# An attention kernel at TensorE's bound: order of cut score products, places of the x load and outputs, start and tail

## The chip, the cores and the metric

The kernel runs on one core of one Trainium2 chip. The metric is the device time of one execution in microseconds (us); lower is better. A median of several executions is quoted for each kernel with its extremes. Ratios are of the mean time of one kernel's fast runs over that of the other's in the same rounds, so they are not quite the ratios of the medians. For kernels that were only looked at (one time, one profile), the state of the run is unknown and no interval exists.

All runs of all kernels in this document gave correct results.

## The reference, cut to what matters

```python
# x: (32, 256, 32, 32): 32 images, 256 channels, S = 1024 positions; 8 heads of 32
xn = group_norm(x, G=32)                       # 8 channels a group
q, k, v = q_w @ xn + q_b, kv_w @ xn + kv_b     # (256, 1024) each
scores = q_h.T @ k_h / sqrt(32)                # per head, positions strictly before only
attn = softmax(scores);  attn[masked] = 0
out = x + attn @ v                             # residual
```

## The kernel before

The 32 images are worked off one behind the other, with 12 visits for each, 384 in all. A visit is one block of scores, one projection of the next image, and the products with v of the visit before. Four heads share TensorE, each in its own 32 rows ("row group"). The parts that the change and the argument touch:

```python
# A score piece is 512 columns; in 4 of 12 visits it is cut into 384 + 128 (two key blocks).
def piece(g, hf, k, part=None):
    d = k - hf * BPH
    if d == 1:
        blocks = [(k, slice(P, HALF), slice(P, HALF)), (k + 2, slice(0, P), slice(3 * P, HALF))]
    ...

def scores(b, full, half, between=()):
    ...
    first = [scores_of((b, half), short[:, j % 2, 1, :], j) for j in (2, 3)]   # 2 short products
    for j in range(4):
        scores_of((b, full), pairs[j // 2][:, j % 2, :], j)    # all blocks of head j inside
    ...                                                        # 2 more short products, then 3 exponentials on ScalarE

# The sums of the exponentials: VectorE adds up pieces (values), two DMAs that add fold them
# to 32 partitions (fold), another stacks four of them (stack), TensorE sums them (pd).
def sum_folded(b):
    pd = misc(f"pd_{b}")
    sum_keys(pd, live.pop(("folded", b)), ..., of_rows=pick_half)
    ...
# Their inverses: 4 DMAs of 256 KB bring them back, spread over partitions
def invert(b, ns):
    ...
    for n in ns:
        nc.sync.dma_start(out=inverses(b, n), in_=by_half[n].unsqueeze(1).broadcast_to([4, HD, HALF]))
# and the outputs use them on VectorE:
def finish(b, n, within=slice(0, HALF)):
    ...
    nc.vector.tensor_mul(rb, num[:, within], rb)                                    # L463
    nc.vector.scalar_tensor_tensor(rb, rb, v_bias_col[...], xt[...], ALU.add, ALU.add)  # L464
    nc.sync.dma_start(out=x_out[b, :, g, cols], in_=rb)

# Which visit does what, relative to the image's first visit (N = 12)
PREPARE = (-18, -17, -9, -9, -8, -8, -7, -6)     # statistics (2), mean, dev, var, rstd, normalised x (2)
FINISH = ((N + 12, N + 12, N + 13, N + 14), ...) # the four outputs
when(max(first - 2 * N + 3, 0), lambda b=b: load(b))
```

`misc` is a single PSUM buffer, which the small products share with some projections. x loads, outputs, stacked sums and inverses all go through the one queue of SyncE, in the order in which they were issued. SyncE waits there for what a transfer needs, and what stands behind waits with it.

## Time and profile before

| | before |
|---|---|
| median of 6 runs | 1877.49 us (1874.42 to 1880.56) |
| profiled execution | span 1874.0 us |
| start until the first score block | 19.02 us |
| an image (12 visits) | 57.20 us |
| cut / whole score block, until the next product | 1.600 / 1.503 us |
| images over 57.2 us | 3 of 29, together 2.3 us over |
| last score block until the end | 23.72 us |

The times in the lower rows are my readings of when each score block starts in the trace; the images are the second to the thirtieth (the first and the thirty-first are longer in both kernels, by 3.5 to 3.9 us). One row of the view of waits matters little at first sight, and much later. Its columns behind the colon are us in total, how many times, and the longest:

```profile
DVE rb L463 <- DMA rb<-inverses: 11.3, 11, 2.5
```

VectorE (DVE) waits 11 times for the fetched inverses before it can compute an output.

### The profile page before, as it was taken

To read this page: it belongs to the slowest core of one execution; us is meant where nothing else is said; L and a number is where in the kernel's file an instruction comes from. 1 tells how busy PE (TensorE), PEld (TensorE's weight loads), DVE (VectorE), ACT (ScalarE), POOL (GpSimd) and SP (SyncE) were. 2 spreads that over 40 slices of the span, in tenths; PEclk is the share of its full clock that TensorE was granted. 3 is DMA by queue.
4 is the path that set the end of the run, shared out by engine and by line. 5 is a ranking of instruction groups with operands and counts; after the bars stand their busy time and mean duration, and the time that the engine had idled before them with its cause. 6 is when DMAs were issued, how large, how long until landed. Compare 5 with 4: busy or idle time off the path is not lost.

```text
span 1874.0 us, 54145 instructions
## 1 busy us (share of the span) xinstructions
PE 1850.8 (99%) x23410; PEld 950.6 (51%) x23410; DVE 1573.4 (84%) x1604; ACT 1413.7 (75%) x1775; POOL 765.5 (41%) x741
## 2 busy tenths in 40 slices
PE   8999999999999999999999999999999999999997
PEld 4555555555554555555555545455555555455543
DVE  3778988888988889888889888898888888888878
ACT  5777777777777777777777777777777777777775
POOL 1443443434434434434344344343343443443413
PEclk9999999999999999999999999999999999999998
DMA  3446665666666666665666656766556666666412
GB/s 119 69 79 144 138 145 118 117 137 138 140 123 127 125 140 139 145 121 111 137 138 142 145 105 123 140 138 148 117 114 140 138 143 116 133 123 140 95 50 81
DMA packets 77516, 233.41 MB, mean 125 GB/s; under 512 B 19808, under 2 KB 20832, under 8 KB 61912
## 3 DMA queue, kind: packets, MB, share of 16 engines
q0 software_dynamic: 15360, 94.39, 34.4%
q1 hardware_dynamic: 60280, 134.72, 24.7%
q8 instruction: 185, 3.03, 0.7%
q10 hardware_dynamic: 1632, 0.79, 0.1%
q14 instruction: 59, 0.48, 0.1%
HBM read 68.41 MB, written 35.62 MB: 56 GB/s over the span
## 4 chain that ended last, share of the span: by engine, by line
PE 97%; DVE 1%; DMA 0%; ACT 0%; issue 0%; ACTq 0%; DVEq 0%
PE sT L277 31%; PE acc L353 26%; PE pp L169 25%; PE ppv L169 13%; PE pd L390 2%; DVE e L358 1%; DMA wn<-in_L_conv_kv_w_dram 0%; DVE rb L464 0%; DVE rb L463 0%; DVE rb L478 0%; ACT e L331 0%; PE pv L169 0%; PE busy L155 0%; ACT k L231 0%; PE pm L169 0%
## 5 line engine op out<-in xcount | busy, mean ns | idle before, releaser
L331 ACT ACTIVATE e<-sT 128x1024 f32<-128x1024 f32 x768 | 748.3, 1022 | 365.4 <-PE sT L277 283.2
L358 DVE TENSOR_TENSOR e<-e,eh 128x1024 f32<-128x1024 f32 x382 | 534.5, 1413 | 247.2 <-PE acc L353 215.1
L292 POOL TENSOR_SCALAR_AFFINE_SELECT e<-e 128x512 f32<-128x512 f32 (+1 forms) x256 | 359.4, 1404 | 678.5 <-ACT e L331 657.9
L358 DVE TENSOR_TENSOR e<-e,e 128x1536 f32<-128x1536 f32 x381 | 618.0, 1622 | 16.9 <-POOL e L292 2.6
L277 PE MATMUL sT<-q,k 32*128 32x256 f32 (+3 forms) x7168 | 617.6, 460 | 0.8 <-ACT k L231 0.8
L277 PEld LDWEIGHTS sT<-q,k 32*128 32x128 f32 x7168 | 463.4, 184 | 163.7 <-ACT q L231 50.6
L169 PE MATMUL pp<-xn,wT 128*32 128x512 f32 x4096 | 492.2, 598 | 0.0
L353 PE MATMUL acc<-e,v 128*32 128x512 f32 (+2 forms) x4096 | 401.1, 486 | 0.0
L329 ACT ACTIVATE eh<-sT 128x1024 f32<-128x1024 f32 x384 | 395.6, 1030 | 0.0
L371 POOL DMA_DIRECT2D e<-e x240 | 199.5, 892 | 388.0 <-PE sT L277 159.5
L169 PE MATMUL ppv<-wT,xn 128*32 128x256 f32 x4096 | 247.3, 382 | 0.0
L353 PEld LDWEIGHTS acc<-e,v 128*32 128x32 f32 x4096 | 132.9, 110 | 223.6 <-issue 201.1
L353 PE MATMUL acc<-eh,v 128*32 128x256 f32 x3072 | 224.4, 379 | 0.0
L169 PEld LDWEIGHTS pp<-xn,wT 128*32 128x32 f32 x4096 | 107.0, 109 | 218.2 <-issue 199.3
L353 PEld LDWEIGHTS acc<-eh,v 128*32 128x32 f32 x3072 | 98.5, 110 | 164.2 <-issue 152.6
L169 PEld LDWEIGHTS ppv<-wT,xn 128*32 128x32 f32 x4096 | 120.2, 109 | 102.0 <-issue 32.1
L292 POOL TENSOR_SCALAR_AFFINE_SELECT eh<-eh 128x512 f32<-128x512 f32 x128 | 160.6, 1255 | 0.1
L464 DVE SCALAR_TENSOR_TENSOR rb<-rb,v_bias_col,x 128x512 f32<-128x512 f32 (+1 forms) x127 | 114.1, 898 | 4.5
L463 DVE TENSOR_TENSOR rb<-num,rb 128x512 f32<-128x512 f32 (+1 forms) x127 | 90.4, 711 | 11.6 <-DMA rb<-inverses 11.3
L231 ACT ACTIVATE k<-pp,qk_bias 128x512 f32<-128x512 f32 x128 | 89.4, 698 | 13.5 <-PE pp L169 12.4
L214 DVE TENSOR_SCALAR xn<-x,mean,rstd 128x512 f32<-128x512 f32 x128 | 96.7, 796 | 2.0 <-POOL rstd L207 2.0
L231 ACT ACTIVATE q<-pp,qk_bias 128x512 f32<-128x512 f32 x128 | 89.9, 702 | 4.0 <-PE pp L169 4.0
(69 smaller groups left out, 515.2 us busy)
## 6 DMA issues: line engine op xcount, KB each, us to landing
e<-e POOLq DMA_DIRECT2D x120, 512.0 KB, 8.0
x<-in_x_dram SPq DMA_DIRECT2D x64, 512.0 KB
out_dram<-rb SPq DMA_DIRECT2D x127, 256.0 KB
rb<-inverses SPq DMA_DIRECT2D x126, 256.0 KB
e<-e POOLq DMA_DIRECT2D x120, 256.0 KB, 5.0
folded<-e SPq DMA_DIRECT2D x120, 256.0 KB
rows<-sums SPq DMA_DIRECT2D x31, 32.0 KB
inverses<-inv SPq DMA_DIRECT2D x31, 32.0 KB
```

Of the source, the lines that this page charges most:

```text
L169: nc.tensor.matmul(out[part], lhsT=lhsT[:, part], rhs=rhs, start=start, stop=stop, skip_group_check=True)
L214: nc.vector.tensor_scalar(live["xn", b][:, g, cols], live["x", b][:, g, cols], mean[:, g : g + 1], rstd[:, g : g + 1], ALU.subtract, ALU.mult,
L231: nc.scalar.activation(live[key][:, cols], pp, AF.Identity, bias=qk_bias[:, n, g : g + 1], scale=(SCALE, 1.0)[n],)
L277: ins = nc.tensor.matmul(pair[:, cols], lhsT=live["k", b, g][rows, kb * P : (kb + 1) * P], rhs=live["q", b, g][rows, hf * HALF + of.start ...
L292: nc.gpsimd.affine_select(out=diagonal, in_=diagonal, pattern=[[0, 4], [0, n], [1, P]], compare_op=ALU.is_gt, fill=0.0, base=0, channel_mu ...
L329: exp = nc.scalar.activation(eh.rearrange("p (n bank) q -> p bank n q", n=2), short, AF.Exp)
L331: nc.scalar.activation(e[:, 2 * a : 2 * a + 2, :], pairs[a], AF.Exp)
L353: nc.tensor.matmul(acc[HD * j : HD * (j + 1), of], lhsT=live["v", b][:, kb, h * HD : (h + 1) * HD], rhs=e[:, j, cols], start=first, stop=l ...
L358: nc.vector.tensor_add(total[:, :, of], total[:, :, of], e[:, :, cols])
L371: nc.gpsimd.dma_start(out=total[:rows], in_=total[rows : 2 * rows], accum_op=ALU.add)
L463: nc.vector.tensor_mul(rb, num[:, within], rb)
L464: nc.vector.scalar_tensor_tensor(rb, rb, v_bias_col[:, g : g + 1], xt[:, g, cols], ALU.add, ALU.add)
```

## The change

Four parts. (1) In cut visits the long pieces of all four heads come first, then the short ones. (2) At the start x of the first image is fetched alone, the weights stand behind it on the same queue, the three weight transposes follow one another, and smaller filler products are to keep TensorE's clock up. (3) At the end one more addition of exponentials is done by TensorE instead of VectorE, the sum that waits for VectorE stands last, and half of the last output goes to GpSimd and ScalarE. (4) In every image the x load goes out three visits later, statistics, the second half of normalised x and the outputs one or two visits later.

```diff
@@ (1) scores
-            for j in range(4):
-                scores_of((b, full), pairs[j // 2][:, j % 2, :], j)
+            for n in range(len(full[4])):
+                for j in range(4):
+                    scores_of((b, full), pairs[j // 2][:, j % 2, :], j, n)
@@ (2) start
-        for b in range(min(2, B)):
-            load(b)
+        load(0)
-                nc.scalar.dma_start(out=live["wn", n], in_=w.rearrange("(o p) c -> p o c", p=P))
+                nc.sync.dma_start(out=live["wn", n], in_=w.rearrange("(o p) c -> p o c", p=P))
-                nc.tensor.matmul(pt[:, 0, :C], lhsT=ident, rhs=live["wn", 0][:, 0, :], start=True, stop=True)
+                nc.tensor.matmul(pt[:, 0, :P], lhsT=ident, rhs=ident, start=True, stop=True)
...
             load_weights()
-            turn_weights(0)
+            if B > 1:
+                load(1)
+            junk = small.tile([P, 1], F32, tag="most", name="junk")
+            nc.scalar.activation(junk, ones, AF.Exp)
+            keep_busy(11)
             for g in range(NG):
                 norm_channels(0, g)
-            keep_busy(2)
+            nc.vector.tensor_scalar_mul(qk_bias[:, 0, :], qk_bias[:, 0, :], SCALE)
             norm_mean(0)
-            turn_weights(1)
+            keep_busy(3)
             ...
-            turn_weights(2)
-            keep_busy(4)
+            for n in range(3):
+                turn_weights(n)
+            keep_busy(3)
@@ (3) tail
-            finish(b, 3, both[0])
+            finish_aside(b, 3, both[0])
...
-                    for pc in products[(i - 1) % N]:
-                        values((i - 1) // N, pc, i < B * N - 1)
+                for n, pc in enumerate(products[(i - 1) % N] if i else ()):
+                    summed = i < B * N - 2 or (i == B * N - 2 and n == 0)
+                    values((i - 1) // N, pc, summed)
+                    if i == B * N:
+                        sum_piece(B - 1, pc, stop=n == 1)
+                        if n == 0:
+                            sum_total(B - 1)
+                if i == B * N - 1:
+                    for n, pc in enumerate(products[N - 2] + products[N - 3][1:]):
+                        sum_piece(B - 1, pc, start=n == 0)
@@ (4) places
-        PREPARE = (-18, -17, -9, -9, -8, -8, -7, -6)
+        PREPARE = (-16, -15, -9, -9, -8, -8, -7, -5)
-        FINISH = ((N + 12, N + 12, N + 13, N + 14), (N + 7, N + 7, N + 8, N + 9))
+        FINISH = ((N + 13, N + 13, N + 14, N + 15), (N + 7, N + 7, N + 8, N + 9))
-                    when(max(first - 2 * N + 3, 0), lambda b=b: load(b))
+                    when(max(first - 2 * N + 6, 0), lambda b=b: load(b))
```

More of the change, by code (lines that the diff above doesn't have):

```diff
@@ L151, in keep_busy @@
         def keep_busy(n):
-            pt = ps_s.tile([P, 2, HALF], F32, tag="sT", name=f"busy_{n}")
+            pt = ps_s.tile([P, 2, HALF], F32, tag="sT", name="busy")
             for _ in range(n):
-                nc.tensor.matmul(pt[:, 0, :C], lhsT=ident, rhs=live["wn", 0][:, 0, :], start=True, stop=True)
+                nc.tensor.matmul(pt[:, 0, :P], lhsT=ident, rhs=ident, start=True, stop=True)
         def spare(name):
@@ L270, in piece, with scores_of @@
             return g, hf, k, part, tuple(blocks)
-        def scores_of(pc, pair, j):
+        def scores_of(pc, pair, j, n=0):
             b, (g, hf, k, part, blocks) = pc
             rows = slice(HD * j, HD * (j + 1))
-            for kb, cols, of in blocks:
-                ins = nc.tensor.matmul(
-                    pair[:, cols], lhsT=live["k", b, g][rows, kb * P : (kb + 1) * P],
-                    rhs=live["q", b, g][rows, hf * HALF + of.start : hf * HALF + of.stop],
-                    start=True, stop=True, skip_group_check=True,
-                )
-            return ins
+            kb, cols, of = blocks[n]
+            return nc.tensor.matmul(
+                pair[:, cols], lhsT=live["k", b, g][rows, kb * P : (kb + 1) * P],
+                rhs=live["q", b, g][rows, hf * HALF + of.start : hf * HALF + of.stop],
+                start=True, stop=True, skip_group_check=True,
+            )
         def mask(pc, e):
@@ L393, in sum_keys, with sum_piece, sum_total @@
                 )
-        def sum_pieces(b, pieces, start, stop):
+        def sum_piece(b, pc, start=False, stop=False):
             if start:
                 live["pd", b] = misc(f"pd_{b}")
-                sum_keys(live["pd", b], live["sum", b, NG - 1, NH - 1], slice(0, HALF), slice(0, HALF), True, False)
-            for pc in pieces:
-                e = live.pop(("e", b, pc))
-                for kb, cols, of in pc[4]:
-                    sum_keys(live["pd", b], e, cols, of, False, stop and pc is pieces[-1])
+            e = live.pop(("e", b, pc))
+            for kb, cols, of in pc[4]:
+                sum_keys(live["pd", b], e, cols, of, start, stop)
+        def sum_total(b):
+            sum_keys(
+                live["pd", b], live["sum", b, NG - 1, NH - 1], slice(0, HALF), slice(0, HALF), False, False
+            )
         def sums(b, g, hf):
             n = NH * g + hf
-            total = live.pop(("sum", b, g, hf))
+            den = small.tile([P, HALF], F32, tag="den", name=f"den_{b}_{n}")
             if (b, n) == (B - 1, 3):
@@ L412, in sums @@
                 pd = misc(f"pd_{b}_{n}")
-                sum_keys(pd, total, slice(0, HALF), slice(0, HALF))
-            den = small.tile([P, HALF], F32, tag="den", name=f"den_{b}_{n}")
+                sum_keys(pd, live.pop(("sum", b, g, hf)), slice(0, HALF), slice(0, HALF))
             if b == B - 1 and n >= 2:
@@ L467, in finish, with finish_aside @@
             nc.sync.dma_start(out=x_out[b, :, g, cols], in_=rb)
+        def finish_aside(b, n, within=slice(0, HALF)):
+            g, hf = divmod(n, NH)
+            cols = slice(hf * HALF + within.start, hf * HALF + within.stop)
+            num, rb, xt = live["num", b, n], live["rb", b, n][:, within], live["x", b]
+            nc.gpsimd.tensor_tensor(rb, num[:, within], rb, ALU.mult)
+            nc.gpsimd.tensor_tensor(rb, rb, xt[:, g, cols], ALU.add)
+            nc.scalar.activation(rb, rb, AF.Identity, bias=v_bias_col[:, g : g + 1])
+            if cols.start == 0:
+                nc.scalar.copy(rb[:, 0:1], xt[:, g, 0:1])
+            nc.sync.dma_start(out=x_out[b, :, g, cols], in_=rb)
         def check_here(n, ok):
@@ L478, in invert_here @@
             nc.vector.reciprocal(rb[:, within], live["den", n][:, within])
-        def finish_aside(b, n):
-            g, hf = divmod(n, NH)
-            cols = slice(hf * HALF, (hf + 1) * HALF)
-            num, rb, xt = live["num", b, n], live["rb", b, n], live["x", b]
-            nc.gpsimd.tensor_tensor(rb, num, rb, ALU.mult)
-            nc.gpsimd.tensor_tensor(rb, rb, xt[:, g, cols], ALU.add)
-            nc.scalar.activation(rb, rb, AF.Identity, bias=v_bias_col[:, g : g + 1])
-            if hf == 0:
-                nc.scalar.copy(rb[:, 0:1], xt[:, g, 0:1])
-            nc.sync.dma_start(out=x_out[b, :, g, cols], in_=rb)
         def end_last(b):
@@ L561, in unshifted @@
             norm_rstd(0)
-            turn_weights(2)
-            keep_busy(4)
+            for n in range(3):
+                turn_weights(n)
+            keep_busy(3)
             for hf in range(NH):
                 norm_apply(0, slice(hf * HALF, (hf + 1) * HALF))
-            nc.vector.tensor_scalar_mul(qk_bias[:, 0, :], qk_bias[:, 0, :], SCALE)
             units = projections(0)
@@ L584, in unshifted @@
                     v = first + (N if last and n == 3 else SUMS[n])
-                    if last and n == 3:
-                        for i in (N - 1, N):
-                            when(first + i, lambda b=b, i=i: sum_pieces(b, products[i - 1], i == N - 1, i == N), after)
                     if late:
@@ L618, in unshifted @@
                     f()
-                if i:
-                    for pc in products[(i - 1) % N]:
-                        values((i - 1) // N, pc, i < B * N - 1)
+                for n, pc in enumerate(products[(i - 1) % N] if i else ()):
[8 more added lines that the diff above has]
+                        sum_piece(B - 1, pc, start=n == 0)
                 for f in after.pop(i, ()):
```

## The prediction

> **What bounds the kernel now.** I read the page's busy times and chain of waits first. They say whether one engine is the bound over the whole span.
>
> ```profile
> PE 1850.8 (99%) x23410; PEld 950.6 (51%) x23410; DVE 1573.4 (84%) x1604; ACT 1413.7 (75%) x1775; POOL 765.5 (41%) x741
> ...
> PE 97%; DVE 1%; DMA 0%; ACT 0%; issue 0%; ACTq 0%; DVEq 0%
> ```
>
> TensorE is busy for 99% of the span and makes 97% of the chain that ended last. So outside the first 19 us and the last 25 us only TensorE's own time counts, and work moved between the other engines is worth nothing as long as it stays late enough. I checked this from the starts of the 384 visits (a visit is one block of scores, then one projection, then the value products of the visit before): 12 visits make one of the 32 images, and an image takes 57.20 us almost every time. Only three of the images from the second on differ: 57.93, 58.63 and 57.32, in sum 2.3 us. So there is one fixed cost per visit. Next I read the timeline of TensorE over a few visits, to see how much of a visit is which product.
>
> ```profile
> 943.08 1.67 PE L277 MATMUL sT<-q,k 32*128 32x256 f32 x24
> 944.68 1.92 PE L169 MATMUL pp<-xn,wT 128*32 128x512 f32 x16
> ...
> 947.83 1.57 PE L277 MATMUL sT<-q,k 32*128 32x256 f32 x16
> 949.33 1.92 PE L169 MATMUL pp<-xn,wT 128*32 128x512 f32 x16
> ```
>
> Columns are start, length, engine, line, product, count. Both score blocks stream the same columns. The x24 one has its long piece cut into 384 and 128 columns, and holds TensorE 944.68 - 943.08 = 1.60 us until the projection begins; the x16 one has it whole, and holds 949.33 - 947.83 = 1.50 us. Over all visits I find 1.600 against 1.503 us, nearly without spread. There are 4 cut visits per image, 128 in all.
>
> Last, I read the chain in order of time at both ends, where TensorE does wait:
>
> ```profile
> 1.82 8.96 DMA wn<-in_L_conv_kv_w_dram
> ...
> 10.83 1.12 PE wt L148 x4
> 11.95 2.69 PE busy L155 x8
> 14.64 3.62 PE pp L169 x32
> ```
>
> The start waits for the third weight matrix, because weights and two images of x are fetched at once; then 8 filler products stand ahead of the first projection.
>
> ```profile
> 1854.07 1.95 DVE e L358
> ...
> 1856.07 3.67 PE pd L390 x24
> 1859.74 1.68 PE acc L353 x24
> 1861.41 1.34 PE pd L390 x24
> ...
> 1867.04 1.68 DVE rb L478
> ```
>
> At the end TensorE waits for VectorE's last addition (L358) before it sums the exponentials (pd), and the final divisions are then serial on VectorE. The table of stretches adds why the 3.67 us are so long:
>
> ```profile
> 1857.00:1860.40 3.40, 3.40 (x28) 1.24 (x24) 3.40 (x2) 0.00 (x0) 3.30 (x3) 0.50 0.12 46
> ```
>
> The third column from the right is the granted clock: it was halved after the 2.05 us wait at 1854 to 1856.
>
> **What the Trainium skill says.** "TensorE: Matmul & The Clock Gate", Part 3, The mechanism, states that a weight load overlaps running products only where the row group differs, and that matmuls start and end strictly in program order. The trace agrees on the first as far as row groups overlap (in the x16 block matmuls of different row groups start 7 ns apart), and contradicts the second: in the x24 block of 943.08 the second 384-column matmul starts 13 ns after the first, while the 128-column one that stands between them in the program starts 0.76 us later. So each row group (one head) works off its own sequence. The same page, Part 1, says that the clock falls to half after an idle window; the stretch above shows 0.50. "DMA: Bandwidth & Descriptors", Issuing engines are not separate DMA queues, says transfers from all queues interleave on the same 16 engines; this trace agrees: x on one queue and weights on another land alternately, x's second half at 6.6, the last weights at 10.8 us. "SBUF — State Buffer", Who interferes with whom, says a VectorE operation with two inputs in SBUF and a GpSimd operation exclude each other; the multiplication L463 takes 0.68 us, but 1.17 us at 1861.12 beside GpSimd's L486.
>
> **The change part by part.**
> (1) Score order. The new order of instructions shows the four heads' 384-column matmuls first, then the four 128-column ones; before, each head's 384 and 128 stood together. Single records of the visit at 943.08 say what that costs. The first short products (heads 2 and 3) hold their row groups until 943.62. The weights for head 2's 384 columns are loaded at 943.41, but those for head 3's only at 943.62, just after head 2's first piece began, although head 3's row group could have taken them at 943.41. Head 3's matmul there is 584 ns long against 481 ns for those with weights in place: 0.103 us of bare weight load. I read this as head 2's second piece standing in front and blocking the issue of head 3's first. In the x16 block, where nothing stands between, both heads load together (952.370 and 952.377). In the new order nothing stands between either, so a cut visit should cost what a whole one does: 1.600 - 1.503 = 0.097 us. Times 128, less the two last ones that wait for ScalarE anyway: 126 x 0.097 = 12.2 us, all on the path. An image becomes 57.20 - 4 x 0.097 = 56.81 us.
> (2) Start. x is fetched alone first, and the weights follow on the same queue. With x undisturbed its second half should land about 1.2 us earlier (estimate: 1 MB at the 340 to 400 GB/s that the packets show, from 2.2 us), so the statistics and normalised x come some 1 us earlier. The weights, 0.75 MB right behind x and ahead of the next image, should be there by 8 to 8.5 us instead of 10.8. The filler ahead of the projection shrinks from 8 records of 256 columns (2.69 us) to 6 of 128, about 0.8 us; but all 12 transposes (1.12 us for each of three groups) now follow one another. From the statistics' second sum at about 9 us: 3 x 1.1 + 0.8 = 4.1, so the first projection at 12 to 13 instead of 14.6. I take 2.2 us.
> (3) Tail. One addition of 1024 elements more (the 1.95 us one) goes to TensorE as four products of 256 columns, 0.43 us; the sum that waits for VectorE moves behind the other products. TensorE no longer idles for 2.05 us and keeps its clock: from 1853.95, 1.7 of pd + 0.97 acc + 0.97 pd + 0.86 total + 0.43 + 0.43 gives 1859.3 against 1862.7. But VectorE still has the 3.34 us reciprocal and two operations beside GpSimd's; it gains 1 to 2 us, and sets the end. One half of the last output goes to GpSimd and ScalarE: 0.42 + 0.48 us off VectorE's serial end, hidden behind its second reciprocal (1.75 us). Together 2.5 us.
> (4) x three visits later, statistics, normalised x and outputs spread. Off the path: the x load moves from 16.8 us after an image's start to about 29, its statistics are due over two visits (some 12 us) later, and its packets ended 5 to 9 us after the issue in most images, 13 us in the worst, which VectorE's slack (84% busy) should absorb. What it can give is the 2.3 us of the three long images: there the x load went out at 19.3 to 20.3 instead of 16.8 us, the transfers of folded sums followed behind it, and the sum over them (pd) started up to 1.41 us late. After the change x stands behind those transfers in the queue. The profiled execution without those is about 1876.05 - 2.3 = 1873.8, close to the fastest of the three timed runs (1874.42), so the median of 1879.02 probably has more of them.
> Sum: 12.2 + 2.2 + 2.5 = 16.9 us, from 1874 to 1879 depending on how many late sums remain: 1857 to 1862.
>
> **Rivals.** (a) The 1.60 us come from the 8 additional weight loads and matmuls as such, not from their order. Then (1) gives nothing and the time is about 1869. For it: there are 8 records more. Against it: three of the four row groups end on time, and only one shows the bare load. (b) ScalarE takes over: a visit's first matmul needs the score buffer that the last exponential of the visit before releases. In the visit at 952.05 that exponential ended at 956.15, 4.10 us in, and the visit lasts 4.22: 0.12 us of room, but that visit isn't shortened. The cut ones fall from 4.744 to 4.65 and have 0.5 us of room. If it bound after all, half of (1) would be lost: 1865. (c) The moved x load now meets other folds (at 29.6 us in an image) and holds up GpSimd's queue, which waited up to 8.8 us for such transfers, and with it the masks. TensorE shows no such wait now, and masks have some 4 us of room; if it happened in every image at 0.3 us, 10 us would go and the time be 1868. (d) All late sums vanish and the start gains 3 us: 1853.
>
> **Range and chances.** I centre on 1858: the fixed gain is well founded, and the late sums probably mostly go. Rivals (a) to (c) are the upper end and beyond, (d) the lower. Faster by 2% would need under 1841.4, 16 us below my centre, more than both ends can give; slower by 2% (over 1916.6) would need a new wait of 58.6 / 384 = 0.15 us in every visit.
>
> **What would show it.** The x24 score blocks should last 1.50 us to the next product, the image 56.8 us, with no weight load standing bare before a 384-column matmul; the first projection at 12 to 13 us; no wait of TensorE for L358 at the end and a granted clock of 1.00 there; no image over 57.2. I am wrong if cut visits stay at 1.60, if TensorE shows new waits for ScalarE or masks, or if images vary more than before.

## The result

The changed kernel takes 1860.22 us in the median of 6 runs (1858.67 to 1861.51), against 1877.49 us in the same rounds; the ratio of fast runs is 0.9909 with an interval of 0.9896 to 0.9922. The profiled execution has a span of 1856.6 us. So the result lies within 2%, 2.2 us from the predicted 1858. The runs also lie closer together: 2.8 us between extremes instead of 6.1.

| profiled execution | before | after | difference |
|---|---|---|---|
| start until the first score block | 19.02 | 16.74 | 2.28 |
| first to last score block | 1831.27 | 1819.06 | 12.21 |
| last score block until the end | 23.72 | 20.80 | 2.92 |
| span | 1874.0 | 1856.6 | 17.4 |
| an image | 57.20 | 56.85 | 0.35 |
| cut score block | 1.600 | 1.512 | 0.088 |
| images over the shortest by over 0.05 us | 3 (2.3 us) | 0 | 2.3 |

The row from first to last score block is made up of 29 images at 0.349 each (10.1 us), the three long images (2.3 us) and the first image (0.3 us), less 0.55 us by which the last image got longer (48.73 to 49.28 us up to its last score block; I did not follow that up).

The page's busy times and its chain by engine, after:

```profile
PE 1838.8 (99%) x23440; PEld 932.9 (50%) x23440; DVE 1556.5 (84%) x1601; ACT 1414.5 (76%) x1777; POOL 774.5 (42%) x743
...
DVE 2%; PE 2%; issue 0%; ACT 0%; DVEq 0%
```

TensorE is still the bound, with 12.0 us less to do and 30 records more. The second line misleads if compared with before's: here the program that follows the chain back stopped at 1766.0 us, so only the last 91 us are in these shares of the span. Busy time and the starts of the visits have to carry the reading.

TensorE's timeline over two visits, one cut and one whole (start, length, engine, line, product, count):

```profile
906.62 1.58 PE L276 MATMUL sT<-q,k 32*128 32x256 f32 x24
908.13 1.92 PE L168 MATMUL pp<-xn,wT 128*32 128x512 f32 x16
911.27 1.57 PE L276 MATMUL sT<-q,k 32*128 32x256 f32 x16
912.77 1.93 PE L168 MATMUL pp<-xn,wT 128*32 128x512 f32 x16
```

The x24 block now holds TensorE 908.13 - 906.62 = 1.51 us until the projection begins, the x16 block 1.50, though the first still has eight records more (four products; the trace has two records of each).

The start, from the timeline:

```profile
5.16 1.29 DVE L178 BATCH_NORM_STATS2 st<-x 128x6 f32<-128x512 f32 x2 [5.16 <-DMA x<-in_x_dram]
7.06 1.29 DVE L178 BATCH_NORM_STATS2 st<-x 128x6 f32<-128x512 f32 x2 [0.37 <-DMA x<-in_x_dram]
10.10 1.53 PE L147 MATMUL wt<-ident,wn 128*128 128x128 f32 x12
11.37 1.92 DVE L213 TENSOR_SCALAR xn<-x,mean,rstd 128x512 f32<-128x512 f32 x4 [1.59 <-POOL rstd L206]
11.46 0.90 PE L154 MATMUL busy<-ident 128*128 128x128 f32 x6
12.29 3.64 PE L168 MATMUL pp<-xn,wT 128*32 128x512 f32 x32
```

The brackets give the wait before an instruction and what ended it. The statistics start at 5.16 and 7.06 us; in before they started at 4.47 and 6.62. So x came later, not earlier. Normalised x is begun at 11.37 (before: 11.41). What is gained stands on TensorE: all 12 transposes in 1.53 us, then 0.83 us of filler (12.29 - 11.46) instead of 2.69, and the first projection at 12.29 instead of 14.57.

The tail, from the chain in order of time (start, length, engine, tile, line):

```profile
1840.29 3.27 DVE rb L493
1843.58 1.68 DVE rb L466
1845.28 1.65 DVE rb L467
...
1848.06 1.67 DVE rb L493
1849.73 1.69 DVE rb L493
```

The chain now runs through VectorE's reciprocals (L493) and one output, as the prediction said: VectorE sets the end, not TensorE. In the table of stretches the third column from the right is the granted clock:

```profile
1842.00:1846.00 4.00, 3.16 (x56) 1.35 (x44) 3.93 (x3) 1.21 (x4) 3.92 (x4) 1.00 0.08 26
```

It is 1.00 where before had 0.50. And VectorE's wait for the inverses has gone. In the page's groups the last column is the idle time in front of a group: 0.1 us over 126 multiplications, where the view of waits gave 11.3 us for the kernel before:

```profile
L466 DVE TENSOR_TENSOR rb<-num,rb 128x512 f32<-128x512 f32 x126 | 87.8, 696 | 0.1
```

### The profile page after: what moved, and what is told of

Same layout as the page of the kernel before. It is cut to its first block, busy times and chain, and to the rows that moved or that the text cites. A ratio compares the mean times of both kernels' runs of the same rounds, so it can differ in the third digit from the quotient of the medians.

```text
span 1856.6 us, 54181 instructions
## 1 busy us (share of the span) xinstructions
PE 1838.8 (99%) x23440; PEld 932.9 (50%) x23440; DVE 1556.5 (84%) x1601; ACT 1414.5 (76%) x1777; POOL 774.5 (42%) x743
## 3 DMA queue, kind: packets, MB, share of 16 engines
q1 hardware_dynamic: 61096, 135.51, 24.7%
## 5 line engine op out<-in xcount | busy, mean ns | idle before, releaser
L359 DVE TENSOR_TENSOR e<-e,eh 128x1024 f32<-128x1024 f32 x381 | 524.0, 1389 | 260.4 <-PE acc L354 186.2
L359 DVE TENSOR_TENSOR e<-e,e 128x1536 f32<-128x1536 f32 x381 | 629.4, 1652 | 15.4 <-POOL e L290 1.0
L290 POOL TENSOR_SCALAR_AFFINE_SELECT e<-e 128x512 f32<-128x512 f32 (+1 forms) x256 | 368.3, 1439 | 617.7 <-ACT e L332 595.1
L276 PE MATMUL sT<-q,k 32*128 32x256 f32 (+3 forms) x7168 | 606.3, 458 | 0.8 <-ACT k L230 0.8
L276 PEld LDWEIGHTS sT<-q,k 32*128 32x128 f32 x7168 | 444.1, 184 | 169.9 <-ACT eh L330 65.6
L290 POOL TENSOR_SCALAR_AFFINE_SELECT eh<-eh 128x512 f32<-128x512 f32 x128 | 165.1, 1289 | 0.1
L467 DVE SCALAR_TENSOR_TENSOR rb<-rb,v_bias_col,x 128x512 f32<-128x512 f32 x126 | 95.9, 761 | 4.5
L466 DVE TENSOR_TENSOR rb<-num,rb 128x512 f32<-128x512 f32 x126 | 87.8, 696 | 0.1
L178 DVE BATCH_NORM_STATS2 st<-x 128x6 f32<-128x512 f32 x128 | 81.8, 681 | 5.5 <-DMA x<-in_x_dram 5.5
```

The source lines that it names most:

```text
L178: nc.vector.bn_stats(st[:, c, :], live["x", b][:, g, c * HALF : (c + 1) * HALF])
L276: return nc.tensor.matmul(pair[:, cols], lhsT=live["k", b, g][rows, kb * P : (kb + 1) * P], rhs=live["q", b, g][rows, hf * HALF + of.start ...
L290: nc.gpsimd.affine_select(out=diagonal, in_=diagonal, pattern=[[0, 4], [0, n], [1, P]], compare_op=ALU.is_gt, fill=0.0, base=0, channel_mu ...
L359: nc.vector.tensor_add(total[:, :, of], total[:, :, of], e[:, :, cols])
L467: nc.vector.scalar_tensor_tensor(rb, rb, v_bias_col[:, g : g + 1], xt[:, g, cols], ALU.add, ALU.add)
```

## The experiments

Names beginning with `a_` are the changed kernel with an edit, those with `b_` the kernel before with one. Each kernel's median is compared with the runs of before in the same call: 1878.03 us (14 runs, for `a_by_head`, `b_long_first`, `a_split23`, `a_split01`), 1878.24 us (one run, for `a_all_cut_long`, `a_all_cut_head`, `b_no_filler`, `a_old_fetch`) and 1877.04 us (27 runs, for the other four). Runs called timed were in the fast state. The readings of the traces in one table:

| kernel | median us | first score block | cut block | an image | long images (us over) | last score block to end |
|---|---|---|---|---|---|---|
| before | 1877.49 | 19.02 | 1.600 | 57.20 | 3 (2.3) | 23.72 |
| after | 1860.22 | 16.74 | 1.512 | 56.85 | 0 | 20.80 |
| a_by_head | 1871.18 | 18.12 | 1.600 | 57.20 | 0 | 21.58 |
| b_long_first | 1876.48 | 19.56 | 1.512 | 56.85 | 8 (13.8) | 23.31 |
| a_split23 | 1861.25 | 18.12 | 1.519 | 56.87 | 0 | 21.56 |
| a_split01 | 1871.12 | 18.04 | 1.600 | 57.20 | 0 | 21.58 |
| a_all_cut_long | 1868.69 | 18.04 | 1.512 | 57.15 | 0 | 19.93 |
| a_all_cut_head | 1893.97 | 18.23 | 1.600 | 57.92 | 0 | 21.36 |
| b_no_filler | 1876.09 | 17.68 | 1.600 | 57.20 | 4 (3.7) | 23.62 |
| a_old_fetch | 1864.24 | 20.99 | 1.512 | 56.85 | 0 | 22.16 |
| a_old_spread | 1873.01 | 18.00 | 1.512 | 56.85 | 8 (14.7) | 20.82 |
| a_old_outputs | 1863.17 | 18.99 | 1.512 | 56.85 | 8 (6.6) | 20.81 |
| a_old_tail | 1863.68 | 18.98 | 1.512 | 56.85 | 0 | 23.48 |
| a_outputs_aside | 1866.44 | 19.03 | 1.512 | 56.85 | 0 | 27.73 |

A median covers several executions (one where the kernel was only looked at), the other columns one profiled execution each.

### a_by_head: the order alone undone

```diff
-            for n in range(len(full[4])):
-                for j in range(4):
+            for j in range(4):
+                for n in range(len(full[4])):
                     scores_of((b, full), pairs[j // 2][:, j % 2, :], j, n)
```

> The changed kernel with only the order of the cut score pieces put back (each head's 384 and 128 columns together). Theory (a head's second piece standing in front keeps the next head's weights from loading): the 128 cut score blocks go from 1.512 back to 1.600 us, an image from 56.85 to 57.20, the time from 1860.2 to about 1871.3. Rival (the steady gain came from the moved loads and outputs, and the order only went along): cut blocks may change but the time stays within 3 us of 1860.

Measured, timed: 1871.18 us (1870.86 to 1872.36, 5 runs), ratio to before 0.9959 (0.9944 to 0.9975). That is 11.0 us more than the changed kernel. Every cut block is back at 1.600 us and every image at 57.20, with the same products, columns and loads. So the order, not the number of products, costs these 0.088 us per cut visit.

### b_long_first: the order alone done

```diff
-            for j in range(4):
-                scores_of((b, full), pairs[j // 2][:, j % 2, :], j)
+            for n in range(len(full[4])):
+                for j in range(4):
+                    scores_of((b, full), pairs[j // 2][:, j % 2, :], j, n)
```

> The kernel before with only the score order of the change. Theory: cut blocks 1.512 us, an image 56.85 us, time 1877.5 - 11 = 1866.5, but single longer images (late sums, up to 1.4 us each) remain because x and the outputs are where they were; start and end as before (first score block at 19.0 us, about 23.7 us from the last score block to the end). Rival: no gain without the other parts, 1877.

Measured, timed: 1876.48 us (1873.56 to 1884.21, 10 runs), ratio 0.9992 (0.9976 to 1.0008). This was the surprise of the study. The cut block is 1.512 us and the usual image 56.85, exactly as in the changed kernel, and yet nothing that the runs can show is gained: the theory's 1866.5 failed, and the time is the rival's. Eight images are long, by 13.8 us in sum, which eats the 11. The view of waits shows where to look:

```profile
DVE rb L463 <- DMA rb<-inverses: 32.8, 25, 2.3
```

VectorE waits 25 times and 32.8 us for the inverses, three times as much as before. The kernels `a_old_spread` and `a_old_outputs` below test whether the new places of outputs and x loads are what removes this.

### a_split23 and a_split01: which two heads need the order

```diff
 a_split23: heads 0 and 1 head by head; heads 2 and 3 long pieces first
+            for j, n in [(j, n) for j in (0, 1) for n in range(several)] + [(j, n) for n in range(several) for j in (2, 3)]:
 a_split01: heads 0 and 1 long pieces first; heads 2 and 3 head by head
+            for j, n in [(j, n) for n in range(several) for j in (0, 1)] + [(j, n) for j in (2, 3) for n in range(several)]:
```

> The changed kernel with heads 0 and 1 head by head (384,128,384,128) and only heads 2 and 3 long pieces first. Theory (heads 2 and 3 are the ones whose row groups already hold a short product, so only head 2's second piece blocks head 3's first): cut blocks stay at 1.512 us and the time at 1860. Rival (each head whose two pieces stand together costs a share): cut blocks near 1.556 us, time near 1866.

> The mirror: heads 0 and 1 long pieces first, heads 2 and 3 head by head. Theory: the whole cost is back, cut blocks 1.600 us, time 1871. Rival (shares): cut blocks near 1.556 us, time near 1866.

Measured, one look each: 1861.25 and 1871.12 us. With heads 2 and 3 ordered, the cut block is 1.519 us and nearly the whole gain is there; with heads 0 and 1 ordered it is 1.600 us and nothing is. The two kernels differ from each other only in the order of the same eight score pieces. What is special about heads 2 and 3 is that each has a short product running in its row group (the two at the head of every block). So the one place that costs is head 2's second piece standing ahead of head 3's first. Why it costs there is my inference from these two runs and the single records quoted in the prediction, as the profile has no view of what waits inside TensorE: a row group would hold one product running and one waiting. Head 2's row group then meets a third, and what stands behind the third in the program is not issued. Heads 0 and 1 begin with empty row groups, and their second piece stands in nobody's way.

### a_all_cut_long and a_all_cut_head: the dose

```diff
+            whole = full[4]
+            if len(whole) == 1:        # cut the whole pieces into 384 + 128 too
+                ...
+            for n in range(2):         # a_all_cut_head: the two loops the other way round
+                for j in range(4):
+                    scores_of((b, cut), pairs[j // 2][:, j % 2, :], j, n)
```

> The changed kernel with the 256 whole long pieces cut into 384 and 128 columns too, long ones of all heads first. Theory (a cut costs only 0.009 us when nothing stands in front: 1.512 against 1.503): every block 1.512 us, time 1860.2 + 256 x 0.009 = 1862.5. Rival (eight more weight loads and products cost by themselves, and the gain of the change had another source): about 0.1 us per newly cut block, 1860 + 25 = 1885.

> The same cuts, but head by head in all 384 blocks. Same number of loads and products as in the run before it. Theory: every block 1.600 us, time 1860.2 + 128 x 0.088 + 256 x 0.097 = 1896.3. Rival (number of loads decides): equal to the run with long pieces first.

Measured, one look each: 1868.69 and 1893.97 us (1862.5 and 1896.3 were expected). All 379 blocks that were read last 1.512 us in one order and 1.600 in the other, with equal numbers of loads and products. The order is then worth 25.3 us between the two kernels, more than twice the 11.0 us of four visits an image; by the blocks alone it would be 379 x 0.088 = 33.4 us. Most of the missing 8.1 us is a cost that only the quicker kernel shows. It came out 6 us above what was expected of it: in every image TensorE waited there for ScalarE before the product of the variance (pv), which needs the single buffer `misc`:

```profile
PEld pv L168 <- ACT v L246: 16.7, 30, 0.6
```

The stretch ahead of pv is 1.549 us against 1.322 in the changed kernel, 0.23 us in each image, about 6.8 us over 30. (With 8 blocks more at 0.009 each, that also makes up its image of 57.15 instead of 56.85.) In `a_all_cut_head` that stretch is 1.290 us. So a shorter block put ScalarE's copy of v, which had had just enough room, onto the path: the mechanism held, its price in this kernel was changed by a neighbour.

### a_old_spread and a_old_outputs: the places of x load, preparation and outputs

```diff
 a_old_spread
-        PREPARE = (-16, -15, -9, -9, -8, -8, -7, -5)
+        PREPARE = (-18, -17, -9, -9, -8, -8, -7, -6)
-                    when(max(first - 2 * N + 6, 0), lambda b=b: load(b))
+                    when(max(first - 2 * N + 3, 0), lambda b=b: load(b))
 a_old_spread and a_old_outputs
-        FINISH = ((N + 13, N + 13, N + 14, N + 15), (N + 7, N + 7, N + 8, N + 9))
+        FINISH = ((N + 12, N + 12, N + 13, N + 14), (N + 7, N + 7, N + 8, N + 9))
```

> The changed kernel with the x load, the statistics, the normalised x and the outputs at their old visits. Theory (in the long images VectorE waited for late inverses before the last output, the x load stood behind that output in the queue and then shared the DMA engines with the folded sums): long images return, 2 to 6 per execution and 0.1 to 1.4 us each, so 1860.2 + 2 to 4 us, with a wider spread of the runs. Rival (the spread gives nothing that a run shows): 1860 and no image over 56.9 us.

> The changed kernel with only the outputs one visit earlier, as before; x load still three visits later. Theory: VectorE waits for inverses again (10 us in all, as in the kernel before), but no x load stands in front of the folded sums, so no or hardly any long image: 1860. Rival (the waits for inverses alone make the late sums): long images as with everything put back, 1862 to 1864.

Measured, five rounds: with all old places 1873.01 us (1867.59 to 1880.18, 22 runs), ratio 0.9977 (0.9966 to 0.9988); with the outputs alone at the old place 1863.17 us (1860.99 to 1866.84, 6 runs), ratio 0.9922 (0.9903 to 0.9941). Part (4), worth 2.3 us in the prediction, is thus worth 1873.01 - 1860.22 = 12.8 us beside the other parts, give or take 3 us by the intervals of the two ratios.

For the outputs' single visit the medians differ by 3.0 us, but the intervals of the ratios overlap; the eight long images of its profile, which is its slowest run, speak for it. Both expectations were too low. `a_old_spread` was to cost 2 to 4 us. In `a_old_outputs` no or hardly any image was to be long; eight are, and the time is the rival's. That kernel does not take the x load out of the way either: the first half of x still goes out right behind the last output, at 18.4 us in the median and 20.4 to 21.7 in the long images, and only its second half behind the folded sums. What the x load and the preparation are worth each was not run.

The waits of VectorE, first with all old places, then with old outputs:

```profile
DVE rb L466 <- DMA rb<-inverses: 39.6, 31, 2.3
```

```profile
DVE rb L466 <- DMA rb<-inverses: 16.4, 14, 2.0
```

How a wait of VectorE, which is 84% busy, reaches TensorE can be followed in the trace. While the score blocks of image n run, VectorE makes the outputs of image n - 2, TensorE adds up the sums of n - 1 (pd), and x of n + 2 is loaded. Here is image 10 of before, one of the three long ones, which begins at 537.33 us. VectorE waits for the last inverse, SyncE sends the output and behind it x, and pd comes 0.71 us late, 0.09 us after the second of the two folded sums has landed at 570.72 (VectorE's and SyncE's timelines, then the chain):

```profile
554.75 0.69 DVE L463 TENSOR_TENSOR rb<-num,rb 128x512 f32<-128x512 f32 x1 [2.02 <-DMA rb<-inverses]
```

```profile
556.25 0.33 SPq L467 DMA_DIRECT2D out_dram<-rb  x1
556.63 2.05 SPq L117 DMA_DIRECT2D x<-in_x_dram  x2
559.61 13.47 SPq L377 DMA_DIRECT2D folded<-e  x2
```

```profile
570.81 1.06 PE pd L390 x8
```

The four fetches of inverses (256 KB each) are issued within 2.5 us; in before they land 6.1, 8.7, 12.0 and 15.0 us after their issue in the median, the last up to 18.5 us. Counted from the start of image n, the last one lands at this time, and VectorE wants it at that (medians of 26 images, the fifth to the thirtieth):

| | lands: median / 90% / latest | wanted |
|---|---|---|
| before | 13.79 / 16.89 / 18.31 | 14.89 |
| b_long_first | 14.03 / 18.08 / 19.92 | 14.98 |
| a_old_spread | 14.48 / 19.01 / 20.09 | 15.11 |
| a_old_outputs | 15.19 / 18.97 / 19.76 | 16.56 |
| after | 15.76 / 19.10 / 19.84 | 20.23 |

Against the earliest use, the last fetch lands too late in 6 of the 26 images of before, in 9 of `b_long_first`, in 12 of `a_old_spread` and in 8 of `a_old_outputs`. Only with all new places does it never: its latest is 0.39 us ahead of the use.

Why the fetches lie that far apart was not tested. My reading of the records: the semaphore of each of the 126 fetches is raised 5 times, once at about 1 us and four times as it lands, that of an x load or an output 16 times; and from the fourth issue until SyncE's next transfer, 3.2 to 3.8 packets of its queue run at once on average. So a fetch seems to use only four of the 16 DMA engines, and the four fetches to follow one another on the same four. Why the slowest tenth lands 3 us or more behind the median stays open.

Where the fetch is late, two things follow. The x load stands behind the last output in SyncE's queue. With the old places it is normally issued 16.8 us after the image's start, and in the long images of before and `b_long_first` at 19.3 to 21.8. The folded sums are then in flight together with it, and land at 32.7 to 34.9 us in the long images of `b_long_first` (28.9 in the median of before), where TensorE wants them (pd) at 32.60. The view of waits names other releasers for most of these pd, but in all seven images of `b_long_first` whose pd is late by over 0.3 us it starts 0.09 to 0.25 us after the last folded sum has landed.

And VectorE is itself late with the deviations that the variance product needs: where TensorE is late at pv, pv starts 0.14 to 0.15 us after them. By the length of the stretch ahead of pd and pv over the usual one, `a_old_spread` loses 9.4 us at pd (up to 2.45 in an image) and 5.1 at pv, `b_long_first` 9.4 and 2.5 (a halved clock from 401.1 to 404.5 us, behind its longest wait, makes most of the rest of its 13.8), `a_old_outputs` 1.9 and 4.6. After the change the x load is issued behind the last folded transfer (median 24.7 against 23.1 us), and the folded sums land at 30.58 at the latest. That the folded sums are late because they share the DMA engines with x is read from this order; no run separates it from other traffic.

### b_no_filler: the filler products at the start left out

```diff
             turn_weights(2)
-            keep_busy(4)
             for hf in range(NH):
```

> The kernel before without the four filler products (8 records) that stand between the last weight transposes and the first projection. Theory (the change's earlier start came from fewer filler products, not from x landing earlier: in the changed kernel the first half of x is used at 5.16 us against 4.47, and normalised x starts at 11.37 against 11.41): first projection at 12.4 instead of 14.6 us, first score block at 16.8 instead of 19.0, time 2.2 us less than before. Rival (the fetch order gave it): first projection stays near 14 us, or the clock is halved in the projection and eats the gain.

Measured, one look: 1876.09 us; the first score block stands at 17.68 us instead of 19.02. From the chain and the table of stretches:

```profile
11.67 5.25 PE pp L169 x32
```

```profile
13.00:16.00 3.00, 3.00 (x24) 0.85 (x20) 2.73 (x6) 0.69 (x1) 0.00 (x0) 0.69 0.87 339
```

The projection begins at 11.67 instead of 14.57 us, 2.9 us earlier, but lasts 5.25 instead of 3.6 us at a granted clock of 0.69 in the stretch shown. So without this filler 1.3 us of the 2.9 remain, in one execution each: the expectation's two sides both came true in part. The span, 1874.0 us, is that of before, as a fourth image was long. The 2.2 us between the two single times (1878.24 for before) decide nothing, as before's runs lie 6 us apart.

### a_old_fetch: transfers of the start in their old places

```diff
-        load(0)
+        for b in range(min(2, B)):
+            load(b)
-                nc.sync.dma_start(out=live["wn", n], ...)
+                nc.scalar.dma_start(out=live["wn", n], ...)
-            if B > 1:
-                load(1)
```

> The changed kernel with the fetch of before: both images of x at once, the weights beside them on ScalarE's queue; filler and order of the start as changed. Theory (fetch order gives nearly nothing): first score block within 0.7 us of 16.74. Rival (weights behind x gave the gain): first score block at 18 to 19 us.

Measured, one look: 1864.24 us, the first score block at 20.99, and so the expectation failed; the rival's 18 to 19 was missed as well. The first statistics start at 4.77 us here, earlier than with weights behind x. But the scaling of the q bias, which the change put ahead of the deviations on VectorE, waits for a bias that now lies behind weights and x:

```profile
11.20 0.17 DVE L564 TENSOR_SCALAR qk_bias<-qk_bias 128x2 f32<-128x2 f32 x1 [2.99 <-DMA qk_bias<-in_L_conv_q_b_dram]
```

It held VectorE for 2.99 us, and from 10.1 to 16.9 us the clock was at half. So the new places of the transfers are needed by the new order of instructions, and don't bring x earlier; what the order of fetching is worth by itself this kernel cannot say.

### The start in all profiles of the changed kernel's start

The start of the changed kernel was profiled in nine other kernels that keep it whole. The first score block stands at 18.0 to 18.2 us in six of them, at 19.0 in three, and at 16.74 only in the changed kernel's own profile. (Before's start was profiled whole once more, in `b_long_first`: 19.56 us.) What differs is the clock. The transposes of `a_by_head`, from TensorE's timeline, and its table of stretches:

```profile
9.95 2.82 PE L147 MATMUL wt<-ident,wn 128*128 128x128 f32 x12
```

```profile
9.60:13.00 3.40, 3.32 (x24) 3.25 (x24) 1.81 (x5) 1.62 (x4) 0.70 (x1) 0.54 1.02 406
```

They take 2.82 us at a granted clock of 0.54, where the changed kernel's profile had 1.53 at full clock. In that profile the clock was full from 7.4 us on, in the three slow ones only from 14.4 us. The program is the same; where the halved stretches fall is not.

### a_old_tail: the old end

```diff
-            finish_aside(b, 3, both[0])
+            finish(b, 3, both[0])
 ... and sum_pieces, with its visits, as before (four products fewer on TensorE, one addition more on VectorE)
```

> The changed kernel with the end of before (sums of the last two visits together behind the wait for VectorE, last output wholly on VectorE). Theory: from the last score block to the end 23.7 us instead of 20.8, clock at 0.50 for one window of 3.4 us while TensorE still has products; 1863. Rival (the end's gain came from the earlier stages): 20.8 us.

Measured, one look: 1863.68 us; from the last score block to the end 23.48 us against 20.80, that is 2.7. TensorE's timeline and the table of stretches:

```profile
1843.09 1.92 PE L391 MATMUL pd<-e,pick 128*32 128x512 f32 x16 [1.34 <-DVE e L359]
```

```profile
1844.50:1848.00 3.50, 3.50 (x64) 1.64 (x56) 3.46 (x2) 0.59 (x1) 3.42 (x4) 1.00 0.09 28
```

The wait for VectorE's addition is back (1.34 us), but the clock stays at 1.00, which was not expected. So a wait of this kind does not always halve the clock. Its length does not explain that: before's wait was longer (2.05 us), but `b_no_filler` has before's end with the same 2.05 us, and its clock stays at 1.00 until 1864.9 us. Where a halved stretch falls varies by execution, as at the start; and it hardly counted here, as `b_no_filler` has 23.62 us from the last score block to the end against 23.72. By the other profiles with the changed end, from 19.93 to 22.16 us, and the three with the old end, 23.31 to 23.72, its gain is between 1 and 4 us with 2 to 3 as the usual case.

### a_outputs_aside: an attempt at something better

All three first outputs of the last image on GpSimd and ScalarE, so that VectorE has only the last, and the first of them two visits earlier:

```diff
-                    when(first + N, lambda b=b: finish(b, 2))
-                    for n in every[:2]:
-                        when(first + N, lambda b=b, n=n: finish_aside(b, n), after)
+                    for n in every[:3]:
+                        when(first + (N if n else N - 2), lambda b=b, n=n: finish_aside(b, n), after)
```

> An attempt at a better end: the third output of the last image goes to GpSimd and ScalarE as the first two do, and the first of them starts two visits earlier, so VectorE has only the last output. In the changed kernel VectorE's two operations for the third output took 1.66 and 1.64 us beside GpSimd instead of 0.68 and 0.75. Theory: VectorE starts the last checks when the sums are there (about 1 us earlier), end 0.9 us earlier, 1859.3. Rival (GpSimd's additional 2.6 us delay the masks or the half output): same or slower by up to 1 us.

Measured, five rounds: 1866.44 us (1866.0 to 1868.04, 6 runs), ratio 0.9943 (0.9924 to 0.9962); worse than the changed kernel by 6.2 us, and its tail is 27.73 us. ScalarE's timeline says why:

```profile
1845.09 0.72 ACT L479 ACTIVATE rb<-rb,v_bias_col 128x512 f32<-128x512 f32 x1 [5.90 <-POOL rb L478]
1845.94 1.93 ACT L332 ACTIVATE e<-sT 128x1024 f32<-128x1024 f32 x2
```

The output's addition stands in front of the last exponentials in ScalarE's program and waited 5.90 us for GpSimd; the exponentials, and all that hangs on them, waited with it, and TensorE's clock was at half from 1847.5 to 1854.3 us. No version that beats the changed kernel was found.

## Why the prediction was right

The total was right (1858 predicted, 1860.2 measured, within the range). Its parts were less so, and two errors cancelled: the order was credited with its gain alone, and part (4) with 2.3 us at most.

**Order of the scores: right in mechanism, a little large.** The step "head 2's second piece standing in front and blocking the issue of head 3's first" fits the undoing (11.0 us), the pair that orders two heads only (nearly all of the gain against none), and the dose. These show that the place in the order costs; how TensorE holds up the issue inside is inferred. The gain per cut visit was 0.088 us, not 0.097, since a cut block keeps 0.009 us over a whole one; an image became 56.85, not 56.81 us, and 126 visits make 11.1 us instead of 12.2. What failed is the words "all on the path": alone, in `b_long_first`, the 11 us are given back by waits of a different origin. They are on the path only beside part (4).

**Part (4): the step that failed.** The prediction called it "Off the path", to give at most "the 2.3 us of the three long images". Between kernels that have everything else, it is worth 12.8 us. The three long images of before were read rightly: a late x load, folded sums behind it, and a late pd, but the reading stopped one link short. The x load was late because the output ahead of it in the queue was, and that one because VectorE waited for the last of four inverse fetches (11.3 us in the waits of before). In before VectorE waited 11 times, and three images became long. Shorter visits bring forward the outputs, which are placed by visit, while the transfers take as long as they did, and eight images become late. That last step is argued: between the median landing and the use the room fell only from 1.10 to 0.95 us, and why the slowest tenth came 1.2 us later in `b_long_first` isn't shown. The size of part (4) does not hang on it.

None of the rivals named it; rival (c) feared the new x load would collide with folds, where in fact it got out of the way of the transfers ahead of pd. The load was to move to about 29 us and went out at 24.7. So the parts do not add up one by one: the order alone gives nothing that can be measured. The places with the old order were run only together with start and tail (`a_by_head`): in the profiles 1829.4 us from first to last score block against 1831.3, 1.9 us; in the timed runs 6.9 us, of which start and tail make 3.0 in the profile. Both together give 11 us more than that. The sum came out right because both were present. The forecast that no image over 57.2 us would be left, and that runs would vary less, held.

**Start: right in size by chance, wrong in its reason.** "With x undisturbed its second half should land about 1.2 us earlier" failed: it was used 0.4 us later, the first half 0.7 (5.16 against 4.47), and normalised x was begun at the same time. (In all profiles the first half is used at 4.47 to 4.87 us with the old fetch and at 5.08 to 5.27 with the new.) The gain came from the filler, from 2.69 to 0.83 us, and from transposes at full clock: all in 1.53 us, where the prediction had 3 x 1.1. Its own sum, 9 + 4.1, gives 13.1 for the first projection and not "12 to 13"; 12.29 was measured. The 2.28 us of the profile are also a lucky execution: in nine other profiles of the same start the first score block stands at 18.0 to 19.0 us, so the usual gain over before's 19.02 is nearer to 1 us, and I would now put it there. Yet the medians differ by 17.3 us, as the two spans do by 17.4. Both profiled executions were quicker than the median of their kernel by about the same: after's took 1858.67 us, the fastest of its six, 1.55 under the median, and before's 1876.05, 1.44 under. For after the start fits that. For before more late sums in the timed runs than in the profiled one would, but the timed runs have no trace.

**Tail: right.** 2.5 us predicted, 2.9 in the profile and 2.7 by undoing it. VectorE sets the end, its L466 and L467 take 1.68 and 1.65 us beside GpSimd. The step about the clock was half wrong: it is 1.00 as forecast, but `a_old_tail` and `b_no_filler` keep 1.00 with the old wait too, so the wait that was "halved after" in before was not enough to halve it.

**Rivals.** (a) that the additional loads cost as such, is excluded by `a_by_head`. (b) that ScalarE takes over, did not come with four cut visits; with twelve, in `a_all_cut_long`, it came in a different place (pv) with 0.23 us an image. (c) and (d) did not come. One reading was slightly off: the 128-column record at 943.08 starts 0.75 us after the first 384-column one, not 0.76.

## What to carry to other kernels

When an instruction stream is cut into pieces for several row groups of TensorE, try orders in which no row group is given a third product while another has none waiting: here the same work took 0.088 us less a visit. For other shapes that is not shown. Before you shorten the bound engine's work, list the transfers that have a fixed duration and are placed relative to that work, and how much room their slowest tenth has; a gain of 11 us was eaten here by fetches that had just been in time. And test a change of several parts both ways, each alone and each undone: the order gained nothing alone and 11 us beside the new places, which were themselves worth 12.8 us beside it.

## What the Trainium skill lacked or had wrong

- "TensorE: Matmul & The Clock Gate", Part 3, The mechanism, says matmuls start and end strictly in program order. In before's cut block the second 384-column matmul started 13 ns after the first, while the one between them in the program started 0.75 us later: across row groups the program's order did not hold.
- The same section says weights are pulled ahead where row groups differ, but no page says what a further product for a busy row group does to the issue of those behind it. The pair `a_split23` and `a_split01` shows that it matters: 1.519 against 1.600 us a block for the same products. The limit of one running and one waiting is inferred.
- "TensorE: Matmul & The Clock Gate", Part 1, says that the clock's window runs freely and that its ramp therefore varies by execution, by half a microsecond for products back to back. The runs agree that it varies; for this start, which has gaps between its products, the effect was larger: the first score block at 16.74, 18.0 to 18.2 or 19.0 us for one and the same start.
- "DMA: Bandwidth & Descriptors" has bandwidths and the latency of a single transfer, and no landing times for several issued together beside other traffic: four fetches of 256 KB issued within 2.5 us landed 6.1, 8.7, 12.0 and 15.0 us later (medians), the last up to 18.5.
